# Transpositions of the norms, one column at a time between products: QKV, projection and MLP of a four-layer kernel

## The chip, the cores and the metric

The kernel runs on one core of a Trainium2 chip. The metric is the device time of one execution in microseconds. The kernel before was timed in three runs, and the median counts. One more execution was recorded by the hardware profiler, and the profile and the trace are of that one. The engines are TensorE (PE; weight loads are listed as PEld), VectorE (DVE), ScalarE (ACT), GpSimd (POOL) and SyncE (SP), which issues most of the DMAs.

## What is computed

Everything is fp32. The input x has 48 x 48 = 2304 tokens of 768 channels and goes through four layers: a transformer block, a spectral layer (FFT, a small MLP on the modes, inverse FFT), a layer of 12 diffusion steps with a convolution, and a second spectral layer. The change touches only the transformer block:

```
xn = layernorm(x, ln1_g, ln1_b)
q, k, v = split(xn @ qkv_w + qkv_b)
attn = softmax((q*scale) @ k.T + rel_h + rel_w)      # 12 heads of 64
x = x + (attn @ v) @ proj_w + proj_b                 # the projection
xn2 = layernorm(x, ln2_g, ln2_b)
h = gelu(xn2 @ mlp_w1 + mlp_b1)                      # 768 -> 3072
x = x + (h @ mlp_w2 + mlp_b2)                        # 3072 -> 768
```

## The kernel before

**Tiling.** The tokens form six blocks of 384 (three row tiles of 128 each), and two blocks form a superblock: there are three. The 768 channels are six columns of 128. Each large product is cut into two by two blocks and computed with seven block products in place of eight. The sums of blocks that this needs are made on VectorE: on the side of the activations by `block_sums` (four additions of 128 x 1152 numbers, L142 to L145), on the side of the weights in advance. A block product with 128 output rows sums three matmuls of 128 x 128 by 128 x 384 in one PSUM bank.

**Norms and transpositions.** `layernorm_rows` normalizes a tile of 128 tokens by 768 channels in place: two statistics (L73), their sum (the aggregate), the variance, a square root on ScalarE (L79), seven small operations with a Newton step for the reciprocal root, and the scaling of the whole tile (L89). `transpose_norm` then turns a block of 384 tokens into the layout that the products need, channels on partitions: for each of the six columns three transpositions on TensorE (L98) into one PSUM bank, and one eviction that applies the norm's gain and bias, on VectorE for odd columns (L100) and on ScalarE for even ones (L102). Its pool of PSUM has two banks.

**QKV.** Superblock after superblock: rows of v, then q and k by pairs of channel columns, seven products a pair. `prepare(sb, half)` makes one block's norm and transpositions. Before the change, `prepare(sb + 1, 0)` was written after pair 3, with the loads of x for the second half behind it, and `prepare(sb + 1, 1)` after the last pair.

**Projection.** `proj_phase` runs over the three superblocks with `rows_in_seven`: seven products of three row tiles each, 21 calls of `between` a superblock. Each product is evicted by VectorE (or once by ScalarE) into the temporaries u and v, or into an output o: L174 makes u, L176 makes v, L178 the outputs, L180 u again. Products 1, 4, 5 and 6 complete an output of 384 rows by 384 columns; then `emit` has GpSimd add x with the bias (L828), and SP stores the sum to `xr_d` in DRAM (L829). Outputs have two buffers (`bufs=2`).

**MLP.** `mlp_phase` loads rows of `xr_d` again (L924), makes the second norms and transpositions of a superblock (`prepare`), its first layer (12 steps f of seven products with weights loaded at L943, products at L959, Gelu on ScalarE) and its second layer (seven products of 12 steps f, L1022). Residuals are loaded from `xr_d` (L997), and GpSimd adds the bias to them (L998). `follow` runs parts of the next layer between products; its constant `f_fw` is loaded at L1639. Before the change, both norms of superblock 0 were written ahead of the first layer, and those of the next superblock in the second layer, ahead of products 4 and 5.

**What sets the order.** The code is written in the Tile framework. Its scheduler reorders instructions by priority and by costs of its own, and fixes an order for every engine[...]. So the place of a call in the code gives an instruction its priority, not its exact place. Buffers are tags in pools with a count of `bufs`; a new tile in a used buffer waits for the last reader of the old one. A pool that is opened after another was closed may take that one's memory, and then its first loads wait for the last use of that memory.

## Time and profile before

| what | us |
|---|---|
| median of three runs | 3623.33 |
| lowest and highest of them | 3620.80 and 3623.38 |
| profiled execution, its own time | 3626.7 |
| its span in the profile | 3624.9 |
| TensorE busy | 3539.1 (98% of the span) |
| VectorE busy | 2002.9 (55%) |
| ScalarE busy | 1138.5 (31%) |
| GpSimd busy | 685.8 (19%) |

The stages in the trace, in us from the start of the span: QKV to about 450, attention to about 1484, projection to 1610, MLP from 1621 to about 2660, then the other layers. A line of a window gives the stretch, its length, and for each engine its busy time and, in brackets, its number of instructions; after them the clock that TensorE was granted, the DMA engines' mean busy share and the GB/s. A line of the chain gives start, duration and what the end of the kernel hung on in that time; "issue" is time in which an engine waited for nothing that the profile shows. A matmul in fp32 leaves two records in the trace, a transposition one.

### The profile page before, as it was taken

The page shows a single profiled execution, that of the slowest core. Times are in us where ns is not written, and L with a number is a line of the kernel's source. Part 1 is how long each engine was busy: PE and PEld are TensorE (multiplying, and loading weights), DVE is VectorE, ACT ScalarE, POOL GpSimd, SP SyncE. Part 2 cuts the span into 40 slices and gives each one's busy share as a digit, 9 for nine tenths or more (in the row PEclk, how much of TensorE's full clock was granted, in tenths as well). Part 3 has the DMA queues.
Part 4 walks back from the last instruction along what each step waited for, and adds up shares of the span by engine and source line. Part 5 has one row for each costly group of instructions (what it writes and reads, how often), then busy time and mean ns, then how long its engine had stood idle before and what let it go on. Part 6 is the DMA issues. An engine that isn't in the chain of part 4 may idle for free.

```text
span 3624.9 us, 52111 instructions
## 1 busy us (share of the span) xinstructions
PE 3539.1 (98%) x20914; PEld 2174.5 (60%) x20914; DVE 2002.9 (55%) x3014; ACT 1138.5 (31%) x1731; POOL 685.8 (19%) x570
## 2 busy tenths in 40 slices
PE   7999999999999999999999999999999998999998
PEld 4666654444444444555555555555578777995685
DVE  6644456767676776564244324233145478994445
ACT  1222244444555554113101210120033365223341
POOL 4211101111111110340000000000023304961131
PEclk9999999999999999999999999999999999999999
DMA  7555555656545443443345334434444303113345
GB/s 248 205 194 173 197 163 164 185 143 157 162 121 151 125 125 86 125 152 125 107 136 174 106 106 140 146 109 123 140 131 105 94 21 104 33 30 101 95 113 157
DMA packets 257371, 477.66 MB, mean 132 GB/s; under 512 B 36031, under 2 KB 209919, under 8 KB 250913
## 3 DMA queue, kind: packets, MB, share of 16 engines
q1 hardware_dynamic: 247152, 453.20, 41.8%
q10 hardware_dynamic: 9968, 21.04, 1.6%
q8 instruction: 168, 2.75, 0.3%
q14 instruction: 83, 0.67, 0.1%
HBM read 330.53 MB, written 143.62 MB: 131 GB/s over the span
## 4 chain that ended last, share of the span: by engine, by line
PE 87%; DVE 4%; DMA 3%; POOL 3%; ACT 2%; issue 1%; SPq 0%; ACTq 0%; DVEq 0%; POOLq 0%
PE p L959 14%; PE p L1022 13%; PE s L623 12%; PE av L654 12%; PE qk L361 6%; PE c L1186 4%; PE v L169 3%; PE s L633 3%; PE pj L169 2%; PE f_z L1594 2%; PE f_z L1595 2%; PE f_x L1559 2%; PE so L1364 2%; PE f_u L1609 2%; POOL t L1287 2%
## 5 line engine op out<-in xcount | busy, mean ns | idle before, releaser
L643 DVE TENSOR_TENSOR acc<-acc,p 128x928 f32<-128x928 f32 (+1 forms) x480 | 560.5, 1168 | 264.1 <-ACT p L635 222.6
L635 ACT ACTIVATE p<-s 128x928 f32<-128x928 f32 (+1 forms) x540 | 505.9, 939 | 492.2 <-PE s L633 470.2
L623 PE MATMUL s<-qt,kv 64*128 64x464 f32 (+1 forms) x2160 | 521.9, 559 | 7.8 <-DMA qt<-q_d 5.7
L1022 PE MATMUL p<-w,h 128*128 128x384 f32 x1512 | 492.7, 486 | 0.0
L654 PE MATMUL av<-p,kv 128*64 128x464 f32 (+1 forms) x2160 | 443.0, 554 | 0.0
L1022 PEld LDWEIGHTS p<-w,h 128*128 128x128 f32 x1512 | 286.2, 190 | 196.9
L633 PE MATMUL s<-bt,oneh 64*128 64x464 f32 (+1 forms) x1080 | 400.9, 731 | 0.7 <-DMA bt<-rh_d 0.7
L654 PEld LDWEIGHTS av<-p,kv 128*64 128x64 f32 x2160 | 147.0, 137 | 262.0 <-issue 250.6
L623 PEld LDWEIGHTS s<-qt,kv 64*128 64x128 f32 x2160 | 203.1, 187 | 164.8 <-issue 153.6
L959 PE MATMUL p<-x2nT,w 128*128 128x384 f32 x864 | 292.7, 488 | 2.8 <-issue 2.8
L1279 PE MATMUL c<-H,bands 128*48 128x96 f32 x5632 | 243.8, 247 | 11.2 <-issue 10.9
L361 PE MATMUL qk<-xnT,wqk 128*128 128x384 f32 x756 | 249.8, 487 | 0.3 <-DMA wqk<-wqk_d 0.3
L1279 PEld LDWEIGHTS c<-H,bands 128*48 128x48 f32 x5632 | 234.5, 123 | 20.7 <-issue 11.3
L959 PEld LDWEIGHTS p<-x2nT,w 128*128 128x128 f32 x864 | 164.8, 191 | 118.3 <-issue 4.6
L959 PE MATMUL p<-xT,w 128*128 128x384 f32 x648 | 220.7, 486 | 0.0
L998 POOL TENSOR_TENSOR rr<-rr,ml_b 128x1152 f32<-128x1152 f32 x12 | 31.8, 2648 | 954.0 <-DMA rr<-xr_d 645.5
L361 PEld LDWEIGHTS qk<-xnT,wqk 128*128 128x128 f32 x756 | 141.4, 190 | 93.3 <-issue 0.9
L954 ACT ACTIVATE h<-h,ml_b 128x384 f32<-128x384 f32 x144 | 88.3, 614 | 345.8 <-DVE h L974 173.6
L1287 POOL TENSOR_TENSOR t<-s,c 128x768 f32<-128x768 f32 x80 | 144.5, 1830 | 182.7 <-DMA bands<-in_bands_dram 171.8
L959 PEld LDWEIGHTS p<-xT,w 128*128 128x128 f32 x648 | 123.1, 190 | 85.9
L633 PEld LDWEIGHTS s<-bt,oneh 64*128 64x128 f32 x1080 | 107.0, 188 | 105.6 <-issue 103.2
L169 PE MATMUL v<-wv,xnT 128*128 128x384 f32 x378 | 133.8, 499 | 0.6 <-DVE xnT L144 0.5
(326 smaller groups left out, 4665.5 us busy)
## 6 DMA issues: line engine op xcount, KB each, us to landing
w<-w1s_d SPq DMA_DIRECT2D x36, 768.0 KB, 4.1
w<-w2s_d SPq DMA_DIRECT2D x36, 768.0 KB, 4.4
w<-w1s_d SPq DMA_DIRECT2D x36, 576.0 KB, 3.7
w<-in_mlp_w_dram SPq DMA_DIRECT2D x27, 768.0 KB, 4.6
wqk<-wqk_d SPq DMA_DIRECT2D x12, 1344.0 KB, 10.9
yu<-f_ys SPq DMA_DIRECT2D x24, 672.0 KB, 3.8
f_yt<-yu SPq DMA_DIRECT2D x20, 720.0 KB, 6.6
yu<-f_us SPq DMA_DIRECT2D x18, 720.0 KB, 4.6
```

The lines of the kernel that those rows point to most:

```text
L169: nc.tensor.matmul(p[:, :TB], lhsT=rhs[n][:, c, t * P : (t + 1) * P], rhs=w[:, c, :], start=c == 0, stop=c == NC2 - 1)
L361: nc.tensor.matmul(p[:, :TB], lhsT=w[:, n, c, :], rhs=ops[sb][n][:, c, :], start=c == 0, stop=c == NC2 - 1)
L623: nc.tensor.matmul(ps[:, s, :n], lhsT=keys[pr % 2][rows, kt * P : (kt + 1) * P], rhs=held(c)[rows, :n], start=True, stop=False)
L633: nc.tensor.matmul(ps[:, s, :n], lhsT=oneh[rows, b % 2, :], rhs=bts[b // 2][rows, j, :n], start=False, stop=True)
L635: nc.scalar.activation(p, ps[:, :, :n], AF.Exp)
L643: nc.vector.tensor_tensor(probs[c], probs[c], p, ALU.add)
L654: nc.tensor.matmul(avs[c][rows, : size(c)], lhsT=vals[pr % 2][:, kt, rows], rhs=p[:, s, :], start=kt == 0, stop=kt == NT - 1)
L959: nc.tensor.matmul(p[:, :TB], lhsT=w[n][:, c, :], rhs=rhs[n][:, c, :], start=c == 0, stop=c == NC2 - 1)
L1022: nc.tensor.matmul(ps[t][:, :TB], lhsT=hs[left, f][:, t * P : (t + 1) * P], rhs=wt[:, f % KW2, :], start=f == 0, stop=f == NF2 - 1)
L1186: nc.tensor.matmul(ps[:K, i, :n], lhsT=v[:, c, tok : tok + K], rhs=w[:, cc, c0 : c0 + n], start=cc == NC - 1, stop=cc == 0)
L1279: nc.tensor.matmul(ps[r0 : r0 + G, k // 4, cols], lhsT=bands[:, n - GC, i, :] if gr else bands0[:, n, i, :], rhs=H[:, n, :, d : d + NPR], ...
L1287: GP.tensor_tensor(t, sc[:, ch], c1[:, m0 : m0 + GC].unsqueeze(2).to_broadcast([P, GC, RR, NPR]), ALU.mult)
```

## The change

`transpose_norm` becomes a generator that stops after each of its six columns; whoever drives it decides where the next column's three transpositions and its eviction are written.

- QKV: the loads of x for both halves of the next superblock are issued together, ahead of q and k. The generator of half 0 is begun after pair 1, that of half 1 after pair 3, and a column is written between products of the following pairs.
- Projection and MLP: the pools of the MLP's norms (`ml_c`, `ml_x`, and `ml_t` with two PSUM banks) are opened before the projection by the new `mlp_norms`. The norms of superblock 0 (blocks 0 and 1) are driven from the projection's `between`, at calls 36 and 43 to 61 (of 63, numbered from 0), block 1's norm starting when three steps of block 0 are done (`in_turn`); what is left is finished after the last product.
- MLP's second layer: the next superblock's norms are begun ahead of products 4 and 5 as before, and their columns are written after the steps f of these products, except step 6, where `follow` stands.

The core of the diff:

```diff
+def finish(steps):
+    for _ in steps:
+        pass
+
+def in_turn(one, other):
+    for n, _ in enumerate(one):
+        yield
+        if n == 2:
+            next(other)
+            yield
+    yield from other
...
             nc.scalar.activation(xnT[:, cc, :], ps[:, :TB], AF.Identity, ...)
+        yield
...
                     if pr > 1 and n in (2, 5):
                         step()
+                    elif sb + 1 < NSB and (pr in (2, 4) and n or pr in (3, 5) and n < 2):
+                        next(norm, None)
...
-                if pr == NC2 and sb + 1 < NSB:
-                    prepare(sb + 1, 0)
-                    load_x(sb + 1, 1)
+                if pr in (1, 3) and sb + 1 < NSB:
+                    norm = prepare(sb + 1, pr // 2)
...
-            if sb + 1 < NSB:
-                prepare(sb + 1, 1)
...
                 if sb + 1 < NSB:
                     load_x(sb + 1, 0)
+                    load_x(sb + 1, 1)
                 q_and_k(sb, lambda q: position_terms(sb, q), advance)
...
-def proj_phase(tc, x, pw, ps_d, proj_b, oT, xr_d):
+def proj_phase(tc, x, pw, ps_d, proj_b, oT, xr_d, norm):
...
+        norm_at = {36, *range(43, 62)}
...
-            rows_in_seven(nc, pm, f"pj_{sb}", rhs, ..., xp, emit)
+            calls = itertools.count(21 * sb)
+
+            def between():
+                if next(calls) in norm_at:
+                    next(norm, None)
+
+            rows_in_seven(nc, pm, f"pj_{sb}", rhs, ..., xp, emit, between)
+        finish(norm)
...
+def mlp_norms(tc, stack, ident, ln_g, ln_b, xr_d):
+    nc = tc.nc
+    cp, xp = (stack.enter_context(tc.tile_pool(name=f"ml_{n}", bufs=bufs, side="left")) for n, bufs in (("c", 1), ("x", 3)))
+    pt = stack.enter_context(tc.tile_pool(name="ml_t", bufs=2, space=PSUM))
+    ...
+    def prepare(sb, half):
+        ...
+        for t in range(3):
+            ...
+            nc.sync.dma_start(xt, xr_d[r0 : r0 + P, :])
+            xhs.append(layernorm_rows(nc, xp, xt, f"ln2_{blk}_{t}"))
+        X, t1, t2, t4 = ops[sb]
+        yield
+        yield from transpose_norm(nc, pt, xhs, X[:, :, half, :], ident, g, b, f"n2_{blk}")
+        if half:
+            ops[sb] = block_sums(nc, X, t1, t2, t4)
...
-            def product(n, left, right):
+            def product(n, left, right, norm=iter(())):
...
                         follow(psum)
+                    else:
+                        next(norm, None)
+                finish(norm)
...
-            if sb + 1 < NTB // 2:
-                prepare(sb + 1, 0)
-            p = product(4, 1, (1, 1))
+            norms = [prepare(sb + 1, half) if sb + 1 < NTB // 2 else iter(()) for half in range(2)]
+            next(norms[0], None)
+            p = product(4, 1, (1, 1), norms[0])
...
-            if sb + 1 < NTB // 2:
-                prepare(sb + 1, 1)
-            for t, p in enumerate(product(5, 0, "T3")):
+            next(norms[1], None)
+            for t, p in enumerate(product(5, 0, "T3", norms[1])):
...
-        prepare(0, 0)
-        prepare(0, 1)
...
+    mlp_stack = ExitStack()
+    mlp = mlp_norms(tc, mlp_stack, ident, a["ln2_g"], a["ln2_b"], xr_d)
+    proj_phase(tc, x, pw, ps_d, a["proj_b"], oT, xr_d, in_turn(*(mlp[-1](0, half) for half in range(2))))
...
+    mlp_phase(tc, mlp, w1s_d, a["mlp_b1"], a["mlp_w2"], w2s_d, a["mlp_b2"], xr_d, xa_d, follow_in)
+    mlp_stack.close()
```

In the kernel after, the lines stand further down: the transpositions at L114, their evictions at L116 and L118, the norm's scaling at L105, the projection's products at L186, its last adds at L846 and stores at L847, the loads ml_x at L934, the MLP's weights at L977 and first products at L993, and f_fw at L1676.

More of the change, by code (lines that the diff above doesn't have):

```diff
@@ L289, in prepare @@
             xhs = [layernorm_rows(nc, xp, Xs.pop(3 * blk + t), f"ln1_{blk}_{t}") for t in range(3)]
-            transpose_norm(nc, pt, xhs, ops[sb][:, :, half, :], ident, g, b, f"n1_{blk}")
+            return transpose_norm(nc, pt, xhs, ops[sb][:, :, half, :], ident, g, b, f"n1_{blk}")
         def sums(sb):
@@ L411, in qkv_phase @@
                 nc.sync.dma_start(w[:, k], wv[:, k * NC2 : (k + 1) * NC2, 2 * C : 2 * C + TB])
-            prepare(0, 0)
+            finish(prepare(0, 0))
             load_x(0, 1)
@@ L419, in qkv_phase @@
             qms, kms = (qp.tile([P, NC, NSB], F32, tag=n, name=n) for n in ("qms", "kms"))
-            prepare(0, 1)
+            finish(prepare(0, 1))
             combine(nc.gpsimd, (w[:, 0], w[:, 1], a21, w[:, 6]), w[:, 3], w[:, 2], w[:, 5], w[:, 4])
@@ L829, in emit @@
                 nc.sync.dma_start(xr_d[rows(n), cols(half)].rearrange("(t p) c -> p t c", p=P), o)
-            rows_in_seven(nc, pm, f"pj_{sb}", rhs, lambda n: w[:, n - 2] if n > 1 else pw[:, n], xp, emit)
+            calls = itertools.count(21 * sb)
+            def between():
+                if next(calls) in norm_at:
+                    next(norm, None)
+            rows_in_seven(nc, pm, f"pj_{sb}", rhs, lambda n: w[:, n - 2] if n > 1 else pw[:, n], xp, emit, between)
+        finish(norm)
 def weight_sums(nc, pool, gate, pw, w1, w2, ps_d, w1s_d, w2s_d):
@@ L883, in weight_sums, with psum, mlp_phase @@
         yield
-def mlp_phase(tc, ident, w1s_d, b1, w2, w2s_d, b2, ln_g, ln_b, xr_d, xa_d, follow_in):
+def mlp_norms(tc, stack, ident, ln_g, ln_b, xr_d):
+    nc = tc.nc
+    cp, xp = (stack.enter_context(tc.tile_pool(name=f"ml_{n}", bufs=bufs, side="left")) for n, bufs in (("c", 1), ("x", 3)))
+    pt = stack.enter_context(tc.tile_pool(name="ml_t", bufs=2, space=PSUM))
+    g = load_cols(nc, cp, ln_g, NC, "ln2_g")
+    b = load_cols(nc, cp, ln_b, NC, "ln2_b")
+    ops = {}
+    def psum(name):
+        return pt.tile([P, 512], F32, tag="t", name=name)
+    def prepare(sb, half):
+        blk = 2 * sb + half
+        if half == 0:
+            ops[sb] = [cp.tile([P, NC, 2, TB], F32, tag="x2nT", name=f"x2nT_{sb}")]
+            ops[sb] += [cp.tile([P, NC2, TB], F32, tag=f"x{n}", name=f"x{n}_{sb}") for n in ("T1", "T2", "T4")]
+        xhs = []
+        for t in range(3):
+            xt = xp.tile([P, C], F32, tag="x", name=f"ml_x_{blk}_{t}", bufs=6)
+            r0 = (3 * blk + t) * P
+            nc.sync.dma_start(xt, xr_d[r0 : r0 + P, :])
[5 more added lines that the diff above has]
+            ops[sb] = block_sums(nc, X, t1, t2, t4)
+    return cp, psum, ops, prepare
+def mlp_phase(tc, opened, w1s_d, b1, w2, w2s_d, b2, xr_d, xa_d, follow_in):
     nc = tc.nc
     V = nc.vector
+    cp, psum, ops, prepare = opened
     with (
-        tc.tile_pool(name="ml_c", bufs=1, side="left") as cp,
-        tc.tile_pool(name="ml_x", bufs=3, side="left") as xp,
         tc.tile_pool(name="ml_w", bufs=4, side="left") as wp,
@@ L901, in mlp_phase @@
         tc.tile_pool(name="ml_m", bufs=6, space=PSUM) as pm,
-        tc.tile_pool(name="ml_t", bufs=2, space=PSUM) as pt,
     ):
-        g = load_cols(nc, cp, ln_g, NC, "ln2_g")
-        b = load_cols(nc, cp, ln_b, NC, "ln2_b")
         b1c = load_cols(nc, cp, b1, NF, "ml_b1")
@@ L908, in mlp_phase @@
         follow = follow_in(x1p)
-        ops = {}
-        def psum(name):
-            return pt.tile([P, 512], F32, tag="t", name=name)
-        def prepare(sb, half):
-            blk = 2 * sb + half
-            if half == 0:
-                ops[sb] = [cp.tile([P, NC, 2, TB], F32, tag="x2nT", name=f"x2nT_{sb}")]
-                ops[sb] += [cp.tile([P, NC2, TB], F32, tag=f"x{n}", name=f"x{n}_{sb}") for n in ("T1", "T2", "T4")]
-            xhs = []
-            for t in range(3):
-                xt = xp.tile([P, C], F32, tag="x", name=f"ml_x_{blk}_{t}", bufs=6)
-                r0 = (3 * blk + t) * P
-                nc.sync.dma_start(xt, xr_d[r0 : r0 + P, :])
-                xhs.append(layernorm_rows(nc, xp, xt, f"ln2_{blk}_{t}"))
-            X, t1, t2, t4 = ops[sb]
-            transpose_norm(nc, pt, xhs, X[:, :, half, :], ident, g, b, f"n2_{blk}")
-            if half:
-                ops[sb] = block_sums(nc, X, t1, t2, t4)
         hs = {}
@@ L1064, in second_layer @@
             store(2)
-        prepare(0, 0)
-        prepare(0, 1)
         for sb in range(NTB // 2):
@@ L1449, in block_kernel @@
     xr_d = dram.tile([T, C], F32, tag="xr_d", name="xr_d")
-    proj_phase(tc, x, pw, ps_d, a["proj_b"], oT, xr_d)
+    mlp_stack = ExitStack()
+    mlp = mlp_norms(tc, mlp_stack, ident, a["ln2_g"], a["ln2_b"], xr_d)
+    proj_phase(tc, x, pw, ps_d, a["proj_b"], oT, xr_d, in_turn(*(mlp[-1](0, half) for half in range(2))))
     pw_close()
@@ L1456, in block_kernel @@
     follow_in = lambda *args: afno_follow(nc, xa_d, a["fw2"], yu, todo, *args)
-    mlp_phase(tc, ident, w1s_d, a["mlp_b1"], a["mlp_w2"], w2s_d, a["mlp_b2"], a["ln2_g"], a["ln2_b"], xr_d, xa_d, follow_in)
+    mlp_phase(tc, mlp, w1s_d, a["mlp_b1"], a["mlp_w2"], w2s_d, a["mlp_b2"], xr_d, xa_d, follow_in)
+    mlp_stack.close()
     xh, xh_close = opened("xh", [P, NC // 2, G * HD], "right")
```

## The prediction

> **What bounds the kernel now.** I read the page first: TensorE is busy for 98% of the span and is most of the chain that ended last. A step is worth something only where TensorE stands still, or where it lengthens what TensorE waits for.

> ```profile
> PE 3539.1 (98%) x20914; PEld 2174.5 (60%) x20914; DVE 2002.9 (55%) x3014; ACT 1138.5 (31%) x1731; POOL 685.8 (19%) x570
> PE 87%; DVE 4%; DMA 3%; POOL 3%; ACT 2%; issue 1%; SPq 0%; ACTq 0%; DVEq 0%; POOLq 0%
> ```

> Next the groups of TensorE, for the transpositions of the two norms (after the bar: busy us, mean ns of one, then idle before them):

> ```profile
> L98 PE MATMUL n_tp<-ident,x 128*128 128x128 f32 x108 | 19.5, 310 | 20.3 <-DVE x L89 18.0 <-ACT xnT L102 1.4 <-DVE xnT L100 0.9
> L98 PE MATMUL n_tp<-ident,ml_x 128*128 128x128 f32 x108 | 16.1, 281 | 2.8 <-ACT x2nT L102 2.8
> ```

> Of the 20.3 us in QKV, 18.0 are the very first norm, which the change leaves alone. What remains is 2.3 us in QKV and 2.8 us in the MLP. Then the windows, for the stages that the change touches (QKV superblock 0's products, QKV 1 and 2, projection and seam, the MLP's first and later layers):

> ```profile
> 45.00:130.00 85.00, 85.00 (x297) 51.42 (x296) 45.93 (x114) 15.33 (x31) 38.42 (x40) 1.00 0.66 231
> 130.00:210.00 80.00, 80.00 (x381) 52.94 (x380) 55.76 (x127) 20.05 (x44) 15.54 (x15) 1.00 0.56 191
> 1484.00:1622.00 138.00, 130.73 (x415) 76.75 (x416) 78.17 (x143) 10.81 (x22) 70.48 (x26) 0.97 0.52 166
> 1622.00:1960.00 338.00, 338.00 (x1068) 199.41 (x1067) 133.84 (x302) 59.20 (x99) 7.85 (x3) 1.00 0.42 135
> ```

> After the length comes PE: full in all but the projection. The kernel's scheduler already slots most norms between products. Only the projection's end is left, so I followed the chain across it:

> ```profile
> 1563.26 44.21 PE pj L169 x137
> 1607.47 3.23 issue
> 1610.70 2.63 POOL pj_o L828
> 1613.32 0.02 issue
> 1613.34 3.35 DMA xr_d<-pj_o
> 1616.69 0.02 issue
> 1616.71 0.03 SPq L1639
> 1616.74 0.03 issue
> 1616.77 2.29 DMA f_fw<-in_fw_dram
> 1619.06 2.26 issue
> 1621.32 3.69 PE p L959 x6
> ```

> The MLP's first product waits not for the transpositions but for its weights. The weights stand in SP's queue behind the last store of the projection and behind the load of f_fw, which waits for that store to land. SP's timeline shows it (start, length, engine, line):

> ```profile
> 1613.34 0.36 SPq L829 DMA_DIRECT2D xr_d<-pj_o  x1
> 1613.75 0.48 SPq L997 DMA_DIRECT2D rr<-xr_d  x1
> 1616.77 0.35 SPq L1639 DMA_DIRECT2D f_fw<-in_fw_dram  x1
> 1617.17 2.12 SPq L943 DMA_DIRECT2D w<-w1s_d  x4
> ```

> So the seam is: last projection product 1609.80; VectorE's add 1610.00 to 1610.5; GpSimd's add to 1613.32; store landed 1616.69; weights issued 1617.17; product 1621.32. That is 11.5 us, and the 36 transpositions of blocks 0 and 1 (1609.80 to 1618.5 on TensorE's timeline) lie inside it, free.

> [...] The trace agrees for SP (f_fw waits 1613.75 to 1616.77, the weights behind it) and shows for VectorE 3.43 us before 1572.40, when an add waits for a store with a block sum behind it. [...] a clock of 0.50 in 1621 to 1625, and the first two MLP products (six matmuls) take 5.46 us where two of the projection's take 3.87. The pause stays, so this stays. [...] the block sum L143 takes 3.42 us at 1619.32 beside GpSimd's add, and 1.36 alone.

> **The change, part by part.**

> QKV: no instruction is added. Norms of superblocks 1 and 2 start after pairs 1 and 3, and x of the second half is loaded earlier. TensorE was full in 45 to 210 us, so nothing is there to save; the one place with stalls (blocks 4 and 5, 226.98 to 234.64, 36 transpositions in 7.66 us against 36 x 0.11 = 3.95) keeps its order in the built program, all but one group. Six loads of 0.39 MB pass ahead of weight loads on SP: about 1.5 us of issue. Cover: six PSUM banks, about 9 us of products. Without it the norms' 2 to 3 us of waiting on VectorE would show. I take 0, and -2.3 (all the stalls) to +3 as bounds.

> MLP, second layers: same transpositions, between the same products, TensorE full before. 0, bounds -0.5 to +1. In both places the change doesn't do what its words say, because the scheduler had done it: a rival for the whole that the seam alone can refute.

> Projection: three things. In the built program the six groups of block 0 stand between products up to the third of the third matrix, and those of block 1 after each product from there to the second of the fifth.
> 1. The 36 transpositions leave the free gap and go before the projection's end: 36 x 0.11 = +3.95 us of TensorE.
> 2. The scheduler now also pulls the norms of blocks 2 and 3, which ran at 1629.4 to 1644.7 under full products, into the projection. On SP their six ml_x loads follow the store of superblock 2's first output o1. That store was issued at 1591.30, and the norm loads at 1536.31 took 4.0 us; so ml_x of block 2 lands at about 1591.7 + 4.0 = 1595.7. On VectorE its statistics stand directly after u2 (1586.79 + 6 groups x 0.33 + 0.5 = 1589.3), ahead of v0, the eviction of n2_1_tp1, and all later outputs. VectorE idles about 6.3 us. TensorE reaches the fourth group of block 1, which needs the bank that this eviction frees, at about 1595.5 and stands until about 1598: 2.3 to 2.9 us.
> 3. From 1595.6 VectorE works back to back. By its rows: 15 adds of projection outputs x 0.47 = 7.05; 5.5 tiles of norms x 2.0 (two statistics of 0.5, the scaling of 0.58, six or seven small ones of 0.07) = 11; three evictions x 0.6 = 1.8; four block sums x 1.27 = 5.1; together 25. Plus 1.3 where a sum meets GpSimd's add (0 to 3.5, since L143 above lost 2.1). So the last output's add ends at 1595.6 + 26.3 = 1621.9, against 1610.5: +11.4. TensorE's own end, 1609.8 + 3.95 + 2.6 = 1616.4, is hidden under it.

> Behind it nothing changes: GpSimd 2.6, store 3.4, f_fw, weights 4.15. So the first MLP product starts at about 1621.3 + 11.4 = 1632.7. The MLP is full, so what VectorE did ahead is not given back: it was covered there. Sum +11.4 with 0 and 0. Bounds of this part: +3.95 + 2.6 = +6.5 (VectorE just keeps up with TensorE) to +15 (sums stretched twice, loads landing 1.5 later).

> On the profiled execution: 3624.9 span + 1.8 around it = 3626.7; the median of the three timed runs is 3623.33, so I add to that: 3634.7. Half a microsecond more for the chains of small operations through ScalarE's square root: **3635.2**. Differences under 0.2% (7.2 us) count as no change.

> **Rivals.**
> A. VectorE keeps up: loads land early enough that the block 2 norms cost no idle time. Then only transpositions count, +3.95, or +6.5 with the pause: 3627.3 to 3629.8, no measurable change. For: VectorE idled 1.4 us of each 1.94 us product. Against: 25 us of work after 1595.6, where TensorE had 14 left. Chance 0.14, with the smaller effects that end there.
> B. The other side: the seam closes. If the first weights come before the projection ends, the 11.5 us gap becomes product time and only the 3.95 us of transpositions are paid: -7.5, 3615.8; with the QKV stalls, 3613.5. It needs the weight load to leave SP at least 4.15 us before the projection's end, 1613.8. Against: in the built order the first weight load stands after the last store and f_fw, as before. Chance 0.08.
> C. More contention: VectorE's sums and norms meet two GpSimd adds, or block 3's loads, which wait for block 1's last transpositions, hold the stores behind them on SP. +15 to +20: 3638 to 3643. For: 4 sums now fall among GpSimd's adds. Against: SP is free again by about 1603, before store o4 is ready at about 1611. Chance 0.18.
> My own case has 0.60 and a range of 3631 to 3640. The 8-in-10 range reaches from A's end with the QKV stalls saved (3627.3 - 2.3 = 3625) to C's: 3625 to 3643. Faster 0.08 (B), same 0.14 (A), slower 0.78 (mine and C).

> **What would show it.** Right: the QKV windows and the MLP windows full as before; in the projection VectorE idle for about 6 us before a statistics instruction released by an ml_x load; TensorE stalled 2 to 3 us at one group of block 1; the last output's GpSimd add at about 1622 instead of 1610.70; the order store, f_fw, weights unchanged, and the first MLP product about 11 us later. Wrong: if ml_x of block 2 lands before 1590 (then A); if weights are issued before the last store (then B); if QKV or MLP windows show TensorE idle by more than 1 us, there is a loss that I put at nothing.

## The result and the profile after

The changed kernel takes 3634.75 us (median of seven runs, 3631.14 to 3642.67). The kernel before, with the runs made beside it, takes 3620.8 us (seven runs, 3616.4 to 3623.48). The ratio is 1.0046, 95% interval 1.0036 to 1.0055: slower by 13 to 20 us. The forecast was 3635.2 us, which was 11.9 us above the median known then. The measured difference of the medians is 13.95 us.

The two profiled executions differ by less: spans of 3632.5 and 3624.9 us, 7.6 apart. So I split them by stage, with marks that both have:

| stretch | before | after | difference |
|---|---|---|---|
| start to the first product of attention | 458.73 | 456.60 | -2.1 |
| attention, to the first product of the projection | 1025.2 | 1020.75 | -4.5 |
| projection, to the first product of superblock 2 | 85.2 | 84.4 | -0.8 |
| **seam**: from there to the first product of the MLP | 52.15 | 65.70 | **+13.55** |
| from there to the end of the span | 2003.6 | 2005.0 | +1.4 |

The change doesn't touch attention. In the executions profiled for this study that stretch takes from about 1020 to 1025 us, in changed and unchanged kernels alike, so the 4.5 us are scatter between executions. The seam is the measure below: it is read within one execution, so the scatter of the other stages doesn't enter it. It has some of its own: of the kernels below that have the same code there, two read 52.15 and 52.45 (before, qkv_only), two 45.45 both (hold_early, proj_hold_early) and two 65.70 and 66.98 (after, proj_only). So a difference of about 1.3 us is within the scatter.

At the seam, the chain of the kernel after (start, duration, what):

```profile
1613.51 3.88 issue
1617.39 2.62 POOL pj_o L846
1620.01 0.02 issue
1620.03 2.97 DMA xr_d<-pj_o
...
1623.15 0.35 SPq L1676
...
1623.56 3.79 DMA w<-w1s_d
1627.35 0.14 issue
1627.49 12.69 PE p L993 x32
```

The links are those of before: last output's addition on GpSimd, store, f_fw, weights, product. Only its beginning moved. GpSimd's addition starts 55.6 us after superblock 2's first product (1561.79); before it was 41.5 us after it (1569.17). From GpSimd on, both take about 10 us. What delayed it is in VectorE's timeline (start, length, line, operation, and in brackets how long VectorE was idle before it and for what). Before, the first addition into v of superblock 2 stood next in VectorE's order and waited only for its product:

```profile
1588.72 0.56 DVE L176 TENSOR_TENSOR pj_v<-pj,pj_u 128x384 f32<-128x384 f32 x1 [1.38 <-PE pj L169]
```

After, statistics of block 2 stand ahead of it:

```profile
1590.19 1.02 DVE L89 BATCH_NORM_STATS2 ln_st<-ml_x 128x6 f32<-128x384 f32 x2 [8.25 <-DMA ml_x<-xr_d]
...
1591.80 0.67 DVE L116 TENSOR_SCALAR x2nT<-n_tp,ln_g,ln_b 128x384 f32<-128x384 f32 x1
...
1605.03 3.31 DVE L162 TENSOR_TENSOR xT<-x2nT,xT 128x1152 f32<-128x1152 f32 x1
...
1616.41 0.55 DVE L195 TENSOR_TENSOR pj_o<-pj,pj_u 128x384 f32<-128x384 f32 x1
```

VectorE stands for 8.25 us before block 2's first statistics. What is behind them in its order waits too: the first addition into v, whose product ended at 1583.62, starts at 1591.38. Then VectorE works without a gap worth naming until the last output at 1616.41. One block sum takes 3.31 us beside GpSimd's addition of 1603.46 to 1607.13, where the one at 1601.55 took 1.36. TensorE's waits in the projection and at the seam show the other side (line, what it waited for, us in total, times, longest):

```profile
PE p L993 <- DMA w<-w1s_d: 13.8, 1, 13.8
PE n_tp L114 <- DVE ln_ve L93: 4.4, 1, 4.4
```

The first line is the gap at the MLP's start; the second is one stall in front of a transposition of block 1, which before did not exist. (The view names the norm's operation L93, which starts at 1592.38; what the stall ends with is the eviction L116 just ahead of it, from 1591.80 to 1592.47, and the next transposition starts at 1592.52. The same stall in x8 below is put down to that eviction.) The stages that I had put at nothing stayed full (stretch, its length, TensorE's busy time):

```profile
45.00:130.00 85.00, 85.00 (x300) 51.61 (x300) 54.17 (x128) 16.68 (x34) 37.46 (x39) 1.00 0.70 243
130.00:210.00 80.00, 80.00 (x378) 52.96 (x377) 48.60 (x109) 18.77 (x40) 17.03 (x15) 1.00 0.55 187
1960.00:2300.00 340.00, 340.00 (x1077) 200.04 (x1076) 104.24 (x183) 47.16 (x81) 10.67 (x4) 1.00 0.40 126
```

The rest of QKV, 210 to 440 us, has TensorE busy for 227.75 us, against 227.88 before; the MLP from 1640 to 1960 us for 319.75, against 320.00.

### The profile page after: what moved, and what is told of

Read it like the earlier page. It is cut to its first block, busy times and chain, and to the rows that moved or that the text cites. A ratio compares the mean times of both kernels' runs of the same rounds, so it can differ in the third digit from the quotient of the medians.

```text
span 3632.5 us, 52106 instructions
## 1 busy us (share of the span) xinstructions
PE 3534.4 (97%) x20914; PEld 2172.9 (60%) x20914; DVE 2006.4 (55%) x3014; ACT 1130.4 (31%) x1723; POOL 687.9 (19%) x570
## 4 chain that ended last, share of the span: by engine, by line
PE 86%; DVE 6%; DMA 3%; ACT 2%; POOL 1%; issue 1%; SPq 0%; ACTq 0%; DVEq 0%; POOLq 0%
PE p L993 13%; PE p L1056 13%; PE s L640 12%; PE av L671 12%; PE qk L378 6%; PE c L1220 4%; PE v L186 3%; PE s L650 3%; DVE s L1333 2%; DVE H L1317 2%; PE f_z L1631 2%; PE f_z L1632 2%; PE f_x L1596 2%; PE so L1398 2%; PE f_u L1646 2%; ACT c L1322 2%
## 5 line engine op out<-in xcount | busy, mean ns | idle before, releaser
L993 PE MATMUL p<-x2nT,w 128*128 128x384 f32 x864 | 293.3, 489 | 13.8 <-DMA w<-w1s_d 13.8
L993 PEld LDWEIGHTS p<-x2nT,w 128*128 128x128 f32 x864 | 165.1, 191 | 129.8 <-issue 16.4
L993 PE MATMUL p<-xT,w 128*128 128x384 f32 x648 | 220.8, 486 | 0.0
L993 PEld LDWEIGHTS p<-xT,w 128*128 128x128 f32 x648 | 123.1, 190 | 85.9
L1631 PE MATMUL f_z<-f_w,f_o 97*96 97x96 f32 x800 | 133.9, 249 | 0.0
```

The lines of the kernel that those rows point to most:

```text
L993: nc.tensor.matmul(p[:, :TB], lhsT=w[n][:, c, :], rhs=rhs[n][:, c, :], start=c == 0, stop=c == NC2 - 1)
L1631: nc.tensor.matmul(out, lhsT=o1[:, j, 1:3, :].rearrange("c r h -> c (r h)"), rhs=w2t[:, b, 0, :], start=True, stop=False)
```

## The experiments

All were compared with the kernel before. The seam is in us, from each one's profile.

| kernel | median us | ratio, 95% interval | seam |
|---|---|---|---|
| before | 3620.5 to 3623.1 | | 52.15 |
| after | 3634.75 | 1.0036 to 1.0055 | 65.70 |
| hold: after, norms of blocks 2 to 5 kept out of the projection | 3626.52 | 1.0008 to 1.0021 | 56.34 |
| early: after, first weights loaded early | 3623.91 | 1.0000 to 1.0017 | 55.54 |
| hold_early: both | 3611.72 | 0.9965 to 0.9985 | 45.45 |
| proj_only: only the projection's part of the change | 3636.43 | 1.0027 to 1.0055 | 66.98 |
| qkv_only: only the QKV part | 3621.23 | 0.9990 to 1.0007 | 52.45 |
| proj_hold_early: hold_early with the projection's part alone | 3611.18 | 0.9969 to 0.9982 | 45.45 |
| b_early: before, first weights early | 3626.98 | 1.0012 to 1.0028 | see text |
| b_early2: the same, other place in memory | 3620.08 | 0.9993 to 1.0009 | see text |
| x8: after, eight buffers for the norms' rows | 3639.36 | 1.0025 to 1.0059 | 69.75 |

**Which part of the change costs.** proj_only takes the changed kernel and writes QKV's and the second layers' norms as before:

```diff
-                if pr in (1, 3) and sb + 1 < NSB:
-                    norm = prepare(sb + 1, pr // 2)
+                if pr == NC2 and sb + 1 < NSB:
+                    finish(prepare(sb + 1, 0))
+                    load_x(sb + 1, 1)
...
-            p = product(4, 1, (1, 1), norms[0])
+            if sb + 1 < NTB // 2:
+                finish(prepare(sb + 1, 0))
+            p = product(4, 1, (1, 1))
```

> The changed kernel with its QKV part and its part in the MLP's second layers undone: only the norms of blocks 0 and 1 stay in the projection. My theory (all of the loss is at the seam): the seam is 65.7 us as in the changed kernel, against 52.15 before, and the time is that of the changed kernel, 1.0036 to 1.0055 of the kernel before. Rival (the QKV or MLP parts cost too): the time is nearer to the kernel before by 3 us or more.

Measured: seam 66.98, ratio 1.0041. The interval is wide, 10 to 20 us, so the time alone doesn't exclude the rival's 3 us. qkv_only is the opposite, the kernel before with the QKV part:

> The kernel before with the QKV part alone. My theory: no difference, the first attention product at 457 to 459 us, ratio within 0.999 to 1.001. Rival (the earlier loads and steps save the 2 us by which attention began earlier in the profile of the changed kernel): first attention product below 457 us and the time 2 us lower.

Measured: first attention product at 457.06 us, ratio 0.9998 (0.9990 to 1.0007), so between 3.6 us saved and 2.5 us lost, the middle near nothing. In kernels with the old and with the new QKV code attention starts at 456.6 to 458.7; of those with the old code, b_early is at 457.53. The 2.1 us of the table above lie within that. So the loss is the projection's part. The second layers were not run alone; proj_only leaves no loss for them that these runs could tell.

**Transpositions or norms.** hold lets the rows of blocks 2 to 5 load only when the MLP has begun:

```diff
             xt = xp.tile([P, C], F32, tag="x", name=f"ml_x_{blk}_{t}", bufs=6)
+            if sb:
+                nc.scalar.copy(xt[:, :1], gates[sb - 1])
...
                         gelu(h11, 0)
+                        if f == 0:
+                            gates[sb] = cp.tile([P, 1], F32, tag="gate", name=f"gate_{sb}")
+                            nc.scalar.copy(gates[sb], h11[:, :1])
```

> The changed kernel, but the loads of the MLP's blocks 2 to 5 write into a buffer only after a small copy that depends on the first Gelu of the MLP (one 128x1 copy per tile on ScalarE), so their norms can't come into the projection. Measure: the seam, from the first product of superblock 2 of the projection to the first product of the MLP; it took 52.15 us before and 65.70 us after. My theory (3.95 us of transpositions on TensorE, the rest from the norms of blocks 2 and 3 in VectorE's queue ahead of the last output): the seam is 56.1 us, 9.6 shorter than in the changed kernel, TensorE's stall of 4.4 us at a transposition is gone, and the time is about 9 us below that of the changed kernel. Rival (the transpositions and the two PSUM banks themselves make the seam longer): it stays above 62 us.

Measured: seam 56.34, time +3 to +8 us instead of +13 to +20. Its waits on TensorE have no line of a transposition any more:

```profile
PE p L996 <- DMA w<-w1s_d: 11.6, 1, 11.6
PE pj L186 <- DVE ln_q L102: 1.0, 1, 1.0
PE pj L186 <- DVE pj_o L195: 0.9, 1, 0.9
```

So of the seam's 13.55 us, 4.2 remain with the transpositions moved and the norms held (36 x 0.11 = 3.95 were expected), and 9.4 went with the norms of blocks 2 and 3. No cost of the two PSUM banks themselves shows: the 0.2 us left over are less than the scatter of the seam. hold takes away the wait for the load and the work of these norms together; it doesn't tell the two apart.

**What the start hangs on.** early splits the MLP's weight buffers into two pools of two, and opens the first in `mlp_norms`, beside the projection:

```diff
+    wp0 = stack.enter_context(tc.tile_pool(name="ml_w0", bufs=2, side="left"))
...
-                    wt = wp.tile([P, 4, NC2, P], F32, tag="w", ...)
+                    wt = (wp1 if f % 2 else wp0).tile([P, 4, NC2, P], F32, tag="w", ...)
```

> The changed kernel, with the MLP's weights in two pools of two buffers in place of one of four; the first pool is opened beside the projection, so the weights of the MLP's first step load ahead of the projection's last store. My theory (weights behind the last store set the start): the first MLP product follows the projection's last product within a microsecond or, if a PSUM bank or GpSimd has to be waited for, within 6 us; the seam is 52 to 58 us instead of 65.70, and the time about 8 to 13 us below that of the changed kernel, about that of the kernel before. Rival (VectorE's late sums and outputs set the start whatever the weights do): the seam stays above 62 us.

Measured: seam 55.54. SP issues the first weights at 1503, and the first product starts at 1620.60. It no longer waits for the store. The profile lists the 3.44 us before it as issue and names no releaser; by the order of times it waits for the last output's addition, which reads the last PSUM bank of the projection:

```profile
1619.94 0.55 DVE L195 TENSOR_TENSOR pj_o<-pj,pj_u 128x384 f32<-128x384 f32 x1
```

That addition gives way to the next operation at 1620.41, 55.35 us after superblock 2's first product; in the changed kernel it was 55.1. VectorE is as late as before; only GpSimd, store, f_fw and weights, 10 us, are gone from the chain. In the run with both edits the first product again starts just after that addition (1607.50 with 0.56 us, product at 1608.16). Both edits together:

> Both edits together: norms of blocks 2 to 5 held back, first weights loaded early. My theory: the seam is 40.6 + 3.95 + some tenths = 45 us, 7 us less than before the change (48 if the first product has to wait for a PSUM bank or for GpSimd), and the time 6 to 9 us below the kernel before, ratio 0.9975 to 0.998. Rival (the MLP's later steps pay back an early start, for instance by waiting for the second step's weights): seam short, but time within 3 us of the kernel before.

Measured: seam 45.45 and 3611.72 us, ratio 0.9975. The chain has no link between the two phases but 0.7 us:

```profile
1593.92 13.55 PE pj L186 x42
1607.46 0.70 issue
1608.16 31.84 PE p L997 x98
```

The seam gives 6.7 us, and with a pause of 0.70 us and a granted clock of 1.00 from 1607 to 1613, the first two products of the MLP take 3.95 us (1608.16 to 1612.11) instead of 5.46: 8.2 in all, against 5 to 13 measured. With the other parts undone:

> The version with held norms and early weights, but with the QKV part and the part in the MLP's second layers undone. My theory: the gain of 8 to 9 us comes from the seam alone, so the time is 3609 to 3615 against 3620.5 before, ratio 0.9968 to 0.9985, and the seam 45.5 us. Rival (the other two parts contribute): the time is 3 us or more above that of the version with them.

Measured: seam 45.45, 3611.18 us, ratio 0.9976. The gain is the seam's. This version and hold_early are both faster than the kernel before; between them there is no difference that these runs can tell.

**The weights without the transpositions.** b_early is the kernel before with the two pools of weights, the new one opened ahead of the norms' pools.

> The kernel before, with only the first weights loaded early. My theory: the 36 transpositions (to 1618.5 on the trace of before) and then the block sums take the place of the weights, so the seam shrinks from 52.15 to 49 to 51 us and the time by 1 to 3 us. Rival (weights alone are the gap): the seam shrinks by 7 us or more without moving any transposition.

Measured: slower, by 4 to 10 us, which neither theory said. The loss isn't at the seam: the fifth product of the MLP starts 61.60 us after superblock 2's first product, against 61.48 before. In the next layer the profile has a wait that no other kernel has, and GpSimd's input to f_o is later too (9.3 us in place of 7.0 in the groups of TensorE):

```profile
PE f_x L1560 <- DMA f_fh<-in_fh_dram: 5.9, 1, 5.9
```

The edit had shifted what lies where: SP issues the load of the constant f_fh at 2632.15 us, where the kernel before issues it at 2599.09. b_early2 opens the new pool behind the norms' pools instead.

> The kernel before with the first weights loaded early, as in the earlier run of that kind, but with the new pool opened behind the norms' pools, so that the memory that the next layer's constants take is as before. My theory: at the seam the third product of the MLP ends no earlier than before the change by more than 2 us, because the block sums stand in the way; the 5.9 us wait for f_fh is gone; time within 3 us of the kernel before. Rival (the weights alone make up the gap): seam shorter by 7 us, time 6 us lower.

Measured: the wait for f_fh is gone, and the ratio is 1.0001 (0.9993 to 1.0009). At the seam TensorE now fits the first two products between the transpositions and then stands:

```profile
1612.55 0.49 PE L98 MATMUL n_tp<-ident,ml_x 128*128 128x128 f32 x3
1618.59 6.62 PE L960 MATMUL p<-xT,w 128*128 128x384 f32 x12 [5.55 <-DVE xT L144]
1625.04 4.03 PE L960 MATMUL p<-x2nT,w 128*128 128x384 f32 x12
```

The block sums follow the transpositions, and the third product needs them. It starts 54.87 us after superblock 2's first product, 2.7 earlier than before (57.61), but with the fourth it takes 6.45 us, where the next two take 3.87; the fifth starts at 61.32 against 61.48. At the seam, early weights alone are worth next to nothing (0.2 us) and moved transpositions alone cost 4; the two together with the norms held save 8.

**A dose of the cause.** x8 changes one number, `bufs=6` to `bufs=8` for ml_x, so that two tiles of block 2 load before the store of o1.

> The changed kernel with eight buffers in place of six for the rows that the MLP's norms read. The first two tiles of block 2 then load ahead of the store of o1, and their norms go through VectorE before the wait; the third tile's load still stands behind that store. My theory (the end of the seam is the end of VectorE's wait plus what it has to do after it): the wait for ml_x stays and ends at the same distance from the start of superblock 2, 28.4 us, but two tiles of about 2 us fewer come after it, so the seam is 61.7 us instead of 65.70 and the time about 4 us lower than the changed kernel's. Rival 1 (only the number of norms in the projection counts, wherever they stand): 65.7 us as before. Rival 2 (the late load is all that counts, and the work after it hides): 65.7 us too if the wait ends at the same place.

Measured: seam 69.75, 4 us longer, not shorter. Both my number and the rivals' were wrong. (The time, ratio 1.0025 to 1.0059, can't be told from the changed kernel's, so the reading rests on the seam.) VectorE's timeline shows why:

```profile
1581.89 0.56 DVE L89 BATCH_NORM_STATS2 ln_st<-ml_x 128x6 f32<-128x384 f32 x1 [10.52 <-DMA ml_x<-xr_d]
...
1597.22 1.02 DVE L89 BATCH_NORM_STATS2 ln_st<-ml_x 128x6 f32<-128x384 f32 x2 [3.74 <-DMA ml_x<-xr_d]
```

The statistics of the early tiles were now put ahead of the additions of o1, and VectorE waited for them there, 10.52 us. So o1 was stored later (SP at 1590.71, 26.7 us after superblock 2's first product instead of 22.3), the third tile behind that store came later still, and its wait ended at 33.2 us in place of 28.4. After it VectorE needed 25.4 us to the last output instead of 26.7, not 4 less. I had left out that moving a waiting instruction forward moves it in front of other work. What holds is the form of the account: the end of VectorE's wait, plus what stands behind it, plus the chain from there to the product (33.2 + 25.4 + 11.2 us here, 28.4 + 26.7 + 10.6 in the changed kernel).

## Why the prediction was right, step by step

- **QKV and second layers at nothing**: right as far as the runs can tell, by qkv_only and proj_only. The scheduler had interleaved them already.
- **Step 1, 36 transpositions, +3.95 us**: right. hold, which has only them, measures +4.2 at the seam.
- **Step 2, VectorE's wait for ml_x**: right in place and cause, too small. Forecast: ready 26.5 us after superblock 2's first product, 6.3 us idle, TensorE stalled 2.3 to 2.9. Measured: 28.4, 8.25 and 4.4. The norm loads were issued 23.1 us after it, not 22.5, and the first took 5.27 us, where I had used 4.0 from one earlier load of the same size. Over the eighteen loads of this kind the trace of the kernel before gives a median of 5.1 us; with that the wait would have been put about 1 us longer. This term is the one that was mis-sized.
- **Step 3, VectorE's work after the wait, 26.3 us**: measured 26.7 (1590.19 to 1616.88). The single stretched sum was 3.31 against 1.36, so the 1.3 us allowed for GpSimd was a little short. The half microsecond added for square roots on ScalarE doesn't show: VectorE has no listed wait for ScalarE in that stretch.
- **The chain behind it unchanged**: right; GpSimd, store, f_fw and weights took 10.1 us against 10.6. early shows that this chain set the start: without it the seam is 10 us shorter, and the product starts as VectorE finishes.
- **The sum**: +11.4 forecast at the seam, +13.55 measured. Nearly all of the difference is the late end of the wait in step 2. That the absolute time came out within half a microsecond, 3635.2 against 3634.75, is luck: the forecast change was 2 us too small (11.9 against 13.95), and the median of before fell by 2.5 us with more runs.
- **TensorE's own end** was put at 6.6 us later and was 11.1 later (51.7 us after superblock 2's first product against 40.6), still ahead of VectorE's last output at 55.1. The 11.1 us are the transpositions (3.95), the stall (4.4) and about 2.7 us of slow clock after it, which I had put at nothing; it is shown below. So the two chains, TensorE's and VectorE's, start from the same wait and end 3 us apart, where I had forecast 5.5. If VectorE had kept up with TensorE, the seam would still have been about 52.15 + 11.1 = 63 us (an estimate from these figures). Less work on VectorE alone could have saved some 2.5 us, so the 4 us that I expected of x8 were too many on this ground too.
- **Two readings of the trace before** were off. The clock was not 0.50 all through 1621 to 1625: it was 0.50 to 1624 and 0.80 in the last microsecond. And it had fallen at 1617.6, while the transpositions still ran and TensorE had stood for 0.76 us at a stretch at most. So in this trace stops shorter than the stall of step 2, put at 2.3 to 2.9 us, came with a slow clock, and that stall should have had a price for one. That the MLP's first products are slow after the change too is right: the first two took 6.07 us (1627.49 to 1633.56), with the clock at 0.50 from 1618.13 to 1631.79. Also, the norms of blocks 2 and 3 ran to 1649.2, not 1644.7; nothing hangs on that.
- **Rival A** (VectorE keeps up, no measurable change) is what hold shows once the norms are held: it names what the change would have cost without the scheduler's move, some 4 us. **Rival B** (the seam closes, -7.5 us) was refused for the right reason: with the weights out of the queue, and only then, hold_early gains 8.75 us by the medians. That the norms must be held as well I had not said: early alone stays at 55.5 us. **Rival C** lay too far: the stores were not held up behind the loads in a way that shows in the chain.

## What to carry to other kernels

Before you fill a gap, find which chain ends last across it: here work that was free in the gap was moved to the full side, while the gap stood on a store, a small load and the weights in one DMA queue. When code is moved, read what the scheduler moves after it: here norms of two later blocks came into VectorE's queue and cost 9.4 us at the seam, since the first of their instructions waited 8.25 us for a load, and the projection's additions behind it waited too (the first into v for 7.8 us after its product's end). Two edits may be worth something only together, and an edit of pools has to be read in the later layers as well, since it can shift what their constants wait for (b_early: TensorE waited 5.9 us for f_fh).

## What the runs showed of the hardware that I had not expected

In a stall of 4.4 us in the middle of the projection TensorE's granted clock fell from 1.00 to 0.50. In the changed kernel TensorE stands from 1588.15; the clock is 1.00 until 1590.83, then 0.50 until 1597.65. The window (the clock is the third figure from the end):

```profile
1592.00:1598.00 6.00, 5.48 (x13) 3.43 (x14) 6.00 (x20) 1.08 (x4) 0.00 (x0) 0.53 0.00 0
```

The product after the stall is slow, as the chain shows:

```profile
1592.53 0.89 PE n_tp L114 x3
1593.42 3.84 PE pj L186 x6
1597.26 0.58 PE n_tp L114 x3
1597.84 1.94 PE pj L186 x6
```

One product (x6) took 3.84 us there and one takes 1.94 at a clock of 1.00; the two groups of transpositions took 0.89 and 0.58, where 0.33 is usual. So the stall cost about 2.7 us on top of itself. A fall came with a shorter stop in the kernel before: TensorE stood for 1.92 us ahead of the projection's first product at 1483.95, the clock was 0.50 from 1484.44 to 1487.86, and the first six products took 1.7 us longer than in the changed kernel (13.57 against 11.85), where the stop was 1.63 us and the clock stayed at 1.00.

Beside GpSimd's additions of 2.6 to 2.9 us, two operations of VectorE on single columns were long: a product of two 128 x 1 columns (L104), 0.15 us elsewhere, took 2.57 us at 1617.45 and 2.56 at 1622.91 in the kernel after. Others kept their time beside such an addition: with GpSimd busy from 1610.87 to 1613.50, one that reads PSUM took 0.54 us (L195 at 1612.10) and one on a single column 0.13 (L93 at 1613.10).
